# Three hundred trial orders for a two-block kernel, and order edges around the scatters of a sequence

## The chip, the cores and the metric

The kernel runs on one core of a Trainium2 chip. The metric is the device time of one execution in microseconds (us), and the time that counts is the median of several executions. One execution was also taken with the hardware profiler. A core has five engines that work through instruction lists of their own: TensorE (PE) for matmuls, VectorE (DVE), ScalarE (ACT), GpSimd (POOL), and SyncE (SP), which here only issues transfers. Engines wait for one another on semaphores, and each executes its list in order.

## The reference

Sixteen sequences of 512 tokens of width 128 pass through two blocks. Each block is an attention and a mixture of eight experts, with a layer norm after each of the four steps:

```python
x = L0_attn_x                                    # 16 x 512 x 128, fp32
x = layernorm(x + L0_attn(x))                    # 16 heads of 64: cumulative sums of gated values
x = layernorm(x + L0_ffn(x))                     # one of 8 experts for each token (argmax), relu
x = layernorm(x + L1_attn(x))                    # 16 heads of 8: softmax with a position bias
x = layernorm(x + L1_ffn(x))                     # shared expert + one of 8 for each token, silu
```

The first attention forms for each head `cumsum(cross * values) * p2e * extra + values * diag` over a matching denominator, and multiplies by an output weight. The second is a softmax over 512 x 512 scores for each of 16 heads. In both mixtures a token goes to the expert with the largest logit, and to it alone.

## The kernel before, in words

**Tiles.** A sequence is held as four tiles of 128 tokens (NT = 4). The first attention works tile by tile (`tile0`): values `pv` (L894), the gated values `ev` (DVE, L907), their cumulative sums `cum` by a triangular matrix (PE, L929), the division `o` in two DVE steps (L941, L945), a transpose `po` (L952), its copy `ot` on ACT (L955) and the output product `y` (L960). From one tile to the next, the last row of `cum` is copied out (`carry`, ACT, L936) and added into `ev` by a transfer that POOL issues (L920); POOL also computes `self` (L913). The second attention goes round by round over four groups of four heads: bf16 scores `s` (PE, L1127 and L1134) whose row maxima DVE takes (`tops`, L1149), then the scores `st` in fp32 (L1190), bias added on DVE (`p`, L1205), exponential on ACT (L1211), and the product `av` with the values (L1220).

**Mixtures.** Sequences go to the mixtures in chunks of 2, 3, 4, 4, 2 and 1. `route` works out on DVE at which row of a list in DRAM each token stands, sorted by expert. `scatter` then writes the tokens to this list: for each sequence four indirect transfers of 128 rows from POOL (the helper's line is L678). `slots` reads the list back in blocks of 128 rows (`xq`, SP, L756), fetches weights of the block's expert by indirect transfers (`ws`, POOL, L678), runs the expert (up products L1012 or L1385, down products `py` L808) and writes results (L798), and `gather` fetches each token's result (`yg`, POOL).

**What sets the order.** Nothing of this is issued as it is written. Each step is an operation in a plan (`Plan.op`): an engine, a cost and a delay given by hand, the buffers it reads and writes, and a due time. `Plan.order` runs a list scheduler over the operations once: whenever an engine is free in its own clock, it takes the operation with the smallest due time that is ready and has buffers. The kinds of buffers are counted there; the PSUM tiles of two banks, of kind "pair", are three. The instructions are emitted in the order of the plan's starts, and `block_kernel` then ties each emitted instruction to the one before it with an edge of order that asks for no semaphore.

**Around the scatters.** In `scatter`, each of the four transfers waits for the list to be zeroed and for the readers of its former content. For all but the first, the program also states that there is no dependency on any scatter sent so far to this list:

```python
                if t:
                    for other in sent:
                        tc.declare_no_dep(inst, other, reason="rows of their own")
```

These are the same instructions that the edges of order tie one to the next.

Of the kernel before, what the change touches and what calls it, by code (L numbers as in the profile page):

```python
# [2 lines left out]

# [1 line left out]

# [15 lines left out]
NT = N // P  # L21
# [14 lines left out]
VW = 9  # L36
EPS = 1e-5
ROUNDS = NG * NT
EARLY = 1.5

INV2PI = 0.15915494309189535
# [27 lines left out]
class Plan:  # L69
# [33 lines left out]
                buf.left += 1  # L103
        return o

    def order(self):
        free, engines = dict(self.room), range(5)
        leaving = {k: 0 for k in free}
        idle = [0.0] * 5
        able = [[] for _ in engines]  # L110
        unstarted = {}
        for o in self.ops:
            for buf in o.bufs:
                unstarted[buf] = unstarted.get(buf, 0) + 1
            if not o.waits:
                able[o.engine].append(o)
        events, now, out = [], 0.0, []
        self.out, self.freekinds = out, free
        while len(out) < len(self.ops):
            for e in engines:  # L120
                if idle[e] > now:
                    continue
                held = {}
                for o in sorted(able[e], key=lambda o: o.key):
                    if o.ready > now + 1e-9:
                        continue
                    need = {}
                    for buf in o.bufs:
                        if not buf.made:
                            need[buf.kind] = need.get(buf.kind, 0) + 1  # L130
                    if all(
                        free[k] >= n and free[k] + leaving[k] - held.get(k, 0) >= n
                        for k, n in need.items()
                    ):
                        break
                    for k, n in need.items():
                        held[k] = held.get(k, 0) + n
                else:
                    continue
                able[e].remove(o)  # L140
                for k, n in need.items():
                    free[k] -= n
                for buf in o.bufs:
                    if not buf.made:
                        buf.made = True
                        o.makes.append(buf)
                    unstarted[buf] -= 1
                    if not unstarted[buf]:
                        leaving[buf.kind] += 1
                out.append(o)  # L150
                o.start = now
                idle[e] = now + o.cost
                heappush(events, (idle[e], len(out), None))
                heappush(events, (idle[e] + o.delay, len(out), o))
                for then in o.then:

                    pass
            if len(out) == len(self.ops):
                break
            assert events, "no operation can start"  # L160
            now = events[0][0]
            while events and events[0][0] <= now + 1e-9:
                _, _, o = heappop(events)
                if o is None:
                    continue
                for then in o.then:
                    then.waits -= 1
                    then.ready = max(then.ready, now)
                    if not then.waits:
                        able[then.engine].append(then)  # L170
                for buf in o.bufs:
                    buf.left -= 1
                    if not buf.left:
                        free[buf.kind] += 1
                        leaving[buf.kind] -= 1
        self.span = now
        return out


# [1 line left out]
def block_kernel(ctx: ExitStack, tc: tile.TileContext, d, out: bass.AP):  # L181
    nc = tc.nc
# [43 lines left out]
    op = plan.op  # L226
    names, listed = {}, {}
    placed, fetched, zeroed, gathered = {}, {}, {}, {}

    def buf(kind, name):  # L230
        pool, shape, dtype, bufs = kinds[kind]
        return Buf(
            kind, lambda: pool.tile(shape, dtype, tag=kind, name=name, bufs=bufs)
        )

    def load(name, shape, src=None, delay=3.4, gate=()):
# [15 lines left out]
        out=tri, in_=ones, compare_op=ALU.is_ge, fill=0.0, base=0,  # L252
# [5 lines left out]
        out=stri, in_=ones, compare_op=ALU.is_ge, fill=0.0, base=-1,  # L258
# [4 lines left out]
        out=flip, in_=ones, compare_op=ALU.is_equal, fill=0.0, base=1 - P,  # L263
# [31 lines left out]
    for i in range(2):  # L295
# [8 lines left out]
        for pads, k, dtype in ((qk_pad, "qk", F32), (qk16_pad, "qk16", BF16)):  # L304
            m = cp.tile([P, 2, N], dtype, tag=f"{k}_pad{i}", name=f"{k}_pad{i}")
# [13 lines left out]
    def tok(ap):  # L319
        return ap.rearrange("p (t w) -> p t w", w=W)  # L320
# [356 lines left out]
    def indirect(out=None, to=None, in_=None, of=None):  # L677
        nc.gpsimd.indirect_dma_start(  # L678
            out, bass.IndirectOffsetOnAxis(to, 0) if to is not None else None,
            in_, bass.IndirectOffsetOnAxis(of, 0) if of is not None else None,  # L680
        )

    def last():
        return list(nc.cur_bb.bb.instructions)[-1]

    def awaits(inst, others):
        for other in others:
            tc.add_manual_dep(
                inst, other.name,
                mybir.DependencyInfo(mybir.DependencyClass.Sync, mybir.DependencyReason.DATA),  # L690
                reason="list of tokens",
            )

    def scatter(which, c, i, src, place, store):

        n = f"{which}_{c}"
        sent, taken = placed.setdefault(n, []), fetched.get(f"{which}_{c - 2}", [])
        before = [f"zeros{which}_{c % 2}"]  # L700
        before += [f"fetched{which}_{c - 2}_{s}" for s in range(0, SLOTS, 4)]

        def send():
            for t in range(NT):
                indirect(
                    out=store[0], to=place()[:, NT * i + t : NT * i + t + 1],
                    in_=tok(src())[:, t, :],
                )
                inst = last()
                if t:  # L710
                    for other in sent:
                        tc.declare_no_dep(inst, other, reason="rows of their own")
                awaits(inst, [zeroed[f"{which}_{c % 2}"], *taken])
                sent.append(inst)

        op(
            POOL, 5.1, send, reads=[src, place, *before, f"token{n}_{i - 1}"],
            writes=[f"token{n}_{i}"], delay=2.5,
        )
# [336 lines left out]
    def attention1(b, x, at):  # L1056
# [99 lines left out]
        def shifted(g):  # L1156

            pm, mx = buf("one", f"pm_{b}_{g}"), buf("mx", f"mx_{b}_{g}")

            def turn():  # L1160
                for it in range(NT):
                    nc.tensor.transpose(pm()[:NG, col(it)], tops[g % 2][:, it, :], ident)

            op(
                PE, 0.5, turn,
                reads=[("tops", g % 2, it, jp) for it in range(NT) for jp in range(2)],
                writes=[pm],
            )
            op(
                ACT, 0.5, lambda: nc.scalar.copy(mx()[:NG], pm()[:NG]), reads=[pm],  # L1170
                writes=[mx],
            )
            op(
                SP, 0.42,
                lambda: nc.sync.dma_start(qk_pad[g % 2][D1 :: 32, 0, :], mx()[:NG]),
                reads=[mx, *[("qk", g % 2, j) for j in range(4)]],
                writes=[("shift", g % 2)], delay=2.4,
            )
# [77 lines left out]
        for it in range(NT):  # L1256
            plan.due = at - NT - EARLY + it
            maxima(0, it)
        plan.due = at - EARLY
        shifted(0)  # L1260
        for g in range(NG):
            more = g + 1 < NG
            acc = buf("one", f"av_{b}_{g}")
            if more:
                plan.due = at + NT * g - EARLY
                spread(g + 1, qk, qk16)
            for t in range(NT):
                plan.due = at + NT * g + t
                weighted(g, t, acc)
                if more:  # L1270
                    plan.due -= EARLY
                    maxima(g + 1, t)
# [210 lines left out]
    def second(c, b0, xs, lg):  # L1483
        for i, x in enumerate(xs):
            at = float(ROUNDS * (b0 + i))
            attention1(b0 + i, x, at)
# [4 lines left out]
    held = [[] for _ in CHUNKS]  # L1491
# [73 lines left out]
    for c, b0 in enumerate(starts):  # L1565
        begin, length = float(ROUNDS * b0), float(ROUNDS * CHUNKS[c])
        lg = buf("lg", f"lg1_{c}")
# [3 lines left out]
        if c + 1 < len(CHUNKS):  # L1571
# [5 lines left out]
            c, b0, held[c], lg, store,  # L1577
            lambda u: begin + length + (ROUNDS * CHUNKS[c + 1] if c + 1 < len(CHUNKS) else 1) * 0.9 * u,
        )


    order = plan.order()
    block = nc.cur_bb.bb.instructions
    mark = len(block)
    for o in order:
        for made in o.makes:
            made.tile = made.make()
        o.emit()
    chain = [i for i in list(nc.cur_bb.bb.instructions)[mark:]]
    for before, then in zip(chain, chain[1:]):  # L1590
        tc.add_manual_dep(
            then, before.name,
            mybir.DependencyInfo(mybir.DependencyClass.NoSync, mybir.DependencyReason.DATA),
            reason="order",
        )


# [84 lines left out]
```

## Time and profile before

| | |
|---|---|
| median of 3 executions | 2499.63 us (2495.47 to 2499.99) |
| the profiled execution's own time | 2567.31 us |
| its span, first to last instruction | 2564.4 us |
| granted PE clock in it, mean | 0.938 |
| PE busy | 2258.0 us (88%) |
| DVE busy | 1934.8 us (75%) |
| ACT busy | 1000.6 us (39%) |
| POOL busy | 731.2 us (29%) |

The profiler's execution is longer than the timed ones by 2.7%. In the rows of the profile, `out<-in` gives the program's names of what an instruction writes and reads, and L and a number its line. A slice row divides the span in 40 equal parts and gives the busy share of each in tenths. A row of waits says who waited for whom, in us, how many times, and the longest. PE and PEld are the matmuls and the loads of their weights, which overlap.[...]

### The profile page before, as it was taken

Reading aid. Unit: us, or ns where it says so; the run is one execution under the profiler, and the core shown is the slowest. Engines: PE = TensorE matmul, PEld = TensorE weight load, DVE = VectorE, ACT = ScalarE, POOL = GpSimd, SP = SyncE. Lnnn points to the kernel's source line nnn. Section 1 sums busy time; section 2 is a strip of 40 time slices with the busy share of each in tenths; the row PEclk is TensorE's granted clock in tenths of the full one; section 3 lists DMA queues with packets and bytes.
Section 4 is the critical chain, followed back from the end, with each engine's and each line's share of the span. In section 5 each row is a group of like instructions: output and inputs, shape, how many; then the busy total and the mean of one; then the engine's idle time right before and its main releaser. Section 6 shows DMA issues by size and latency. Waiting matters only on the chain.

```text
span 2564.4 us, 33958 instructions
## 1 busy us (share of the span) xinstructions
PE 2258.0 (88%) x12820; PEld 1125.6 (44%) x12820; DVE 1934.8 (75%) x3030; ACT 1000.6 (39%) x1336; POOL 731.2 (29%) x763
## 2 busy tenths in 40 slices
PE   5978889899997997899889988899999889998974
PEld 4556424344553443355434423454344235443443
DVE  5455787897786789777778798778887886789761
ACT  6323144533433543333335443334454333444330
POOL 1244322323223244312132343212213323223232
PEclk9999889999998998898989998999999899998886
DMA  7613113112011331211023411122223112332332
GB/s 179 196 37 101 29 51 90 42 32 75 16 44 52 99 99 30 62 54 41 10 55 102 113 39 46 40 68 70 54 63 90 52 41 74 113 104 62 90 102 88
DMA packets 152438, 179.96 MB, mean 70 GB/s; under 512 B 19332, under 2 KB 125444, under 8 KB 152276
## 3 DMA queue, kind: packets, MB, share of 16 engines
q1 hardware_dynamic: 125588, 84.27, 12.5%
q0 software_dynamic: 26688, 93.53, 12.2%
q8 instruction: 101, 1.65, 0.3%
q14 instruction: 61, 0.50, 0.1%
HBM read 127.67 MB, written 42.93 MB: 67 GB/s over the span
## 4 chain that ended last, share of the span: by engine, by line
PE 58%; DVE 26%; ACT 5%; issue 5%; DMA 2%; another core or an unknown queue 2%; POOL 1%; SPq 0%; DVEq 0%; POOLq 0%; ACTq 0%
PE st L1190 9%; DVE p L1205 9%; PE av L1220 7%; PE s L1127 5%; DVE tops L1149 5%; PE y L960 4%; PE cum L929 4%; PE pv L894 4%; PE s L1134 3%; PE py L808 3%; ACT p L1211 2%; PE po L952 2%; PE pg L1385 2%; DVE o L941 2%
## 5 line engine op out<-in xcount | busy, mean ns | idle before, releaser
L1211 ACT ACTIVATE p<-p 128x1024 f32<-128x1024 f32 x512 | 539.4, 1058 | 539.0 <-DVE p L1205 480.8
L1205 DVE TENSOR_TENSOR p<-st,bias 128x1024 f32<-128x1024 f32 x512 | 606.0, 1216 | 126.1 <-PE st L1190 95.7
L1149 DVE TENSOR_REDUCE tops<-s 128x2 f32<-128x1024 f32 x512 | 604.7, 1215 | 72.5 <-PE s L1134 48.2
L1190 PE MATMUL st<-qk_pad 32*128 32x512 f32 x2048 | 385.2, 663 | 35.6 <-DVE p L1205 20.6
L678 POOL DMA_INDIRECT ws<-tab,rows x212 | 207.6, 979 | 678.9 <-PE py L808 317.8
L1127 PE MATMUL s<-bias,ident 128*128 128x512 bf16 x1024 | 329.4, 403 | 64.0 <-DVE p L1205 37.1
L1220 PE MATMUL av<-p,vaug 128*32 128x512 f32 x2048 | 291.6, 641 | 21.2 <-ACT p L1211 18.2
L913 POOL TENSOR_TENSOR self<-ev,own 128x1024 f32<-128x1024 f32 x64 | 122.6, 1917 | 514.5 <-DVE ev L907 283.7
L1134 PE MATMUL s<-qk_pad 32*128 32x512 bf16 x1024 | 207.0, 397 | 4.1 <-DMA qk_pad<-qk 4.0
L1190 PEld LDWEIGHTS st<-qk_pad 32*128 32x128 f32 x2048 | 113.5, 189 | 190.2 <-issue 70.5
L1127 PEld LDWEIGHTS <-ident 128*128 128x128 bf16 x1024 | 82.3, 99 | 234.6 <-issue 226.4
L678 POOL DMA_INDIRECT yg<-results,place x128 | 126.4, 988 | 141.2 <-issue 46.0
L1134 PEld LDWEIGHTS <-qk_pad 32*128 32x128 bf16 x1024 | 48.8, 91 | 244.2 <-issue 232.9
L929 PE MATMUL cum<-ev,tri 128*128 128x512 f32 x256 | 133.1, 647 | 10.2 <-DVE p L1205 5.1
L960 PEld LDWEIGHTS y<-ow,ot 128*128 128x128 f32 x1024 | 125.6, 197 | 32.8 <-issue 15.2
L960 PE MATMUL y<-ow,ot 128*128 128x128 f32 x1024 | 131.3, 283 | 3.2 <-ACT ot L955 2.6
L894 PE MATMUL pv<-vw,xt 128*128 128x512 f32 x256 | 130.1, 634 | 3.7 <-DVE p L1205 1.9
L941 DVE TENSOR_TENSOR o<-cum,gg 128x1024 f32<-128x1024 f32 x64 | 78.2, 1222 | 68.0 <-PE cum L929 53.2
L808 PEld LDWEIGHTS py<-ws,h 128*128 128x128 f32 x848 | 101.8, 195 | 36.2 <-DVE h L1309 14.4
L907 DVE TENSOR_TENSOR ev<-pv,ex 128x1024 f32<-128x1024 f32 x64 | 78.0, 1220 | 51.6 <-PE pv L894 45.3
L808 PE MATMUL py<-ws,h 128*128 128x128 f32 x848 | 111.2, 285 | 6.3 <-DVE h L1309 5.3
L952 PE MATMUL po<-ident,o 128*128 128x128 f32 x512 | 72.0, 286 | 36.7 <-DVE o L945 30.8
(189 smaller groups left out, 2757.0 us busy)
## 6 DMA issues: line engine op xcount, KB each, us to landing
xq<-tokens SPq DMA_DIRECT2D x44, 256.0 KB
results<-yq SPq DMA_DIRECT2D x44, 256.0 KB
qk_pad<-qk SPq DMA_DIRECT2D x256, 32.0 KB
slid<-line SPq DMA_DIRECT2D x16, 448.0 KB
tokens<-zero SPq DMA_DIRECT2D x4, 1472.0 KB
xt<-in_xt SPq DMA_DIRECT2D x16, 256.0 KB
x<-in_x SPq DMA_DIRECT2D x16, 256.0 KB
qk_pad<-qk SPq DMA_DIRECT2D x256, 16.0 KB
```

The costliest lines, as they stand in the source:

```text
L678: nc.gpsimd.indirect_dma_start(out, bass.IndirectOffsetOnAxis(to, 0) if to is not None else None, in_, bass.IndirectOffsetOnAxis(of, 0) if ...
L808: nc.tensor.matmul(py()[:, col(s)], h()[:, c, col(s)], ws[s]()[:, off + c * W : off + (c + 1) * W], start=(c == 0), stop=(c == 1),)
L894: nc.tensor.matmul(pv()[:, hf, :], xt()[:, col(t)], vw[:, hf * N : (hf + 1) * N], start=True, stop=True,)
L929: nc.tensor.matmul(cum()[:, hf, :], tri, ev()[:, hf, :], start=True, stop=True)
L960: nc.tensor.matmul(y()[:, :P], ot()[:, hf, col(c)], ow[:, 4 * hf + c, :], start=(hf == 0 and c == 0), stop=(hf == 1 and c == 3),)
L1127: nc.tensor.matmul(s()[:, i, :], ident16, bias16[:, 4 * g + 2 * jp + i, 2 * u + 1 : 2 * (u + N) : 2], start=True, stop=False,)
L1134: nc.tensor.matmul(s()[:, i, :], pad[r, 0, col(it)], pad[r, 1, :], start=False, stop=True,)
L1149: lambda s=s, jp=jp: nc.vector.tensor_reduce(tops[g % 2][:, it, 2 * jp : 2 * jp + 2], s(), AX.X, ALU.max, negate=True,),
L1190: nc.tensor.matmul(s[jp]()[:, i, :], pad[r, 1, col(jt)], pad[r, 0, :], start=True, stop=True,)
L1205: lambda jp=jp, h=h, pj=pj: nc.vector.tensor_tensor(pj(), s[jp](), bias[:, h : h + 2, u : u + N], ALU.add),
L1211: ACT, 1.0, lambda pj=pj: nc.scalar.activation(pj(), pj(), AF.Exp),
L1220: nc.tensor.matmul(acc()[32 * j : 32 * j + 32, :], va[:, jt, h * VW : h * VW + 32], p[j // 2]()[:, j % 2, :], start=(jt == 0), stop=(jt == ...
```

## The change

First, the scheduler is split. `listed(keys)` is the list scheduler as before, taking one key for each operation; it works on indices for speed, and returns the starts, or None if nothing can start. `order` calls it with the due times, and then 300 times (TURNS) with keys made from the starts of the list kept so far. In turn 0 they are those starts themselves. In every other turn a stretch of the plan's clock of 30, 100 or 300 is drawn, and in it either single operations (2, 10 or 30% of them), each by an amount of its own, or all operations of one kind by one amount are moved, by up to 2.4, 8 or 24. The new list is kept if the plan's span is not longer. No operation, cost, delay, buffer or due time is changed, and the draw has a fixed seed. Operations that start at the same time are now emitted by engine.

Second, in `scatter` the statement that there is no dependency is kept among the four transfers of a sequence only, and each of the four waits for the four of the sequence before (`sent[-NT:]`). When the edges of order are made, the four count as one member of the chain: each of them is tied to all of the member before and the member after, and they are not tied to one another.

```diff
+TURNS, SHIFT = 300, 8.0
...
+        start = self.listed([o.key[0] for o in ops])
+        best, draw = span(start), Random(0)
+        kinds_of = [o.emit.__code__ for o in ops]
+        for turn in range(TURNS):
+            width, by = draw.choice((30.0, 100.0, 300.0)), SHIFT * draw.choice((0.3, 1.0, 3.0))
+            low = draw.uniform(-width / 2, best)
+            one, share = kinds_of[draw.randrange(len(ops))], draw.choice((0.02, 0.1, 0.3))
+            same, single = draw.uniform(-by, by), draw.random() < 0.5
+            keys = list(start)
+            for i, t in enumerate(start) if turn else ():
+                if low < t < low + width:
+                    if single:
+                        if draw.random() < share:
+                            keys[i] += draw.uniform(-by, by)
+                    elif kinds_of[i] is one:
+                        keys[i] += same
+            other = self.listed(keys)
+            if span(other) <= best:
+                start, best = other, span(other)
+        self.span = best
+        out = sorted(ops, key=lambda o: (start[place[o]], o.engine))
...
         def send():
+            before, row = sent[-NT:], []
             for t in range(NT):
...
-                if t:
-                    for other in sent:
-                        tc.declare_no_dep(inst, other, reason="rows of their own")
-                awaits(inst, [zeroed[f"{which}_{c % 2}"], *taken])
-                sent.append(inst)
+                for other in row:
+                    tc.declare_no_dep(inst, other, reason="rows of their own")
+                awaits(inst, [zeroed[f"{which}_{c % 2}"], *taken, *before])
+                row.append(inst)
+            sent.extend(row)
+            for inst in row:
+                together[inst.name] = row
...
-    chain = [i for i in list(nc.cur_bb.bb.instructions)[mark:]]
+    chain = []
+    for i in list(nc.cur_bb.bb.instructions)[mark:]:
+        row = together.get(i.name, [i])
+        if i is row[0] or i.name == row[0].name:
+            chain.append(row)
     for before, then in zip(chain, chain[1:]):
-        tc.add_manual_dep(
-            then, before.name,
+        for a in before:
+            for b in then:
+                tc.add_manual_dep(
+                    b, a.name,
```

More of the change, by code (lines that the diff above doesn't have):

```diff
@@ L1 @@
+from bisect import insort
 from contextlib import ExitStack
 from heapq import heappop, heappush
+from random import Random
 import numpy as np
@@ L104, in op, with listed @@
         return o
[L106 to L121, printed above, removed]
+    def listed(self, keys):
+        free = [self.room[k] for k in self.kinds]
+        soon = list(free)
+        ops, n = self.ops, len(self.ops)
+        cost, delay, engine, bufs = self.costs, self.delays, self.engines, self.uses
+        kind, then = self.kind, self.thens
+        waits, left, begin = list(self.waiting), list(self.users), list(self.users)
+        made = [False] * len(kind)
+        able = [[] for _ in range(5)]
+        for i in range(n):
+            if not waits[i]:
+                able[engine[i]].append((keys[i], i))
+        for a in able:
+            a.sort()
+        idle, events, now, start, done = [0.0] * 5, [], 0.0, [0.0] * n, 0
+        look = [True] * 5
+        while True:
+            for e in range(5):
+                if idle[e] > now or not look[e]:
@@ L122, in order @@
                     continue
[L123 to L126, printed above, removed]
+                held, pick, line = {}, -1, able[e]
+                for q, (_, i) in enumerate(line):
                     need = {}
-                    for buf in o.bufs:
-                        if not buf.made:
-                            need[buf.kind] = need.get(buf.kind, 0) + 1
+                    for b in bufs[i]:
+                        if not made[b]:
+                            need[kind[b]] = need.get(kind[b], 0) + 1
@@ L131, in order @@
                     if all(
-                        free[k] >= n and free[k] + leaving[k] - held.get(k, 0) >= n
-                        for k, n in need.items()
+                        free[k] >= m and soon[k] - held.get(k, 0) >= m
+                        for k, m in need.items()
                     ):
+                        pick = q
                         break
-                    for k, n in need.items():
-                        held[k] = held.get(k, 0) + n
-                else:
+                    for k, m in need.items():
+                        held[k] = held.get(k, 0) + m
@@ L139, in order @@
+                if pick < 0:
+                    look[e] = False
                     continue
[L140 to L158, printed above, removed]
+                i = line.pop(pick)[1]
+                for b in bufs[i]:
+                    k = kind[b]
+                    if not made[b]:
+                        made[b] = True
+                        free[k] -= 1
+                        soon[k] -= 1
+                    begin[b] -= 1
+                    if not begin[b]:
+                        soon[k] += 1
+                        look = [True] * 5
@@ L159, in order @@
+                start[i] = now
+                done += 1
+                idle[e] = now + cost[i]
+                heappush(events, (idle[e], done, -1 - e))
+                heappush(events, (idle[e] + delay[i], done, i))
+            if done == n:
                 break
-            assert events, "no operation can start"
+            if not events:
+                return None
             now = events[0][0]
             while events and events[0][0] <= now + 1e-9:
-                _, _, o = heappop(events)
-                if o is None:
+                i = heappop(events)[2]
+                if i < 0:
+                    look[-1 - i] = True
@@ L165, in order @@
                     continue
[L166 to L176, printed above, removed]
+                for t in then[i]:
+                    waits[t] -= 1
+                    if not waits[t]:
+                        insort(able[engine[t]], (keys[t], t))
+                        look[engine[t]] = True
@@ new lines, in listed, with order, span @@
+                for b in bufs[i]:
+                    left[b] -= 1
+                    if not left[b]:
+                        free[kind[b]] += 1
+                        look = [True] * 5
+        return start
+    def order(self):
+        ops, place, bufs = self.ops, {}, []
+        for i, o in enumerate(ops):
+            place[o] = i
+        number = {}
+        for o in ops:
+            for b in o.bufs:
+                if b not in number:
+                    number[b] = len(bufs)
+                    bufs.append(b)
+        self.kinds = sorted(self.room)
+        self.kind = [self.kinds.index(b.kind) for b in bufs]
+        self.users = [b.left for b in bufs]
+        self.uses = [[number[b] for b in o.bufs] for o in ops]
+        self.thens = [[place[t] for t in o.then] for o in ops]
+        self.waiting = [o.waits for o in ops]
+        self.costs, self.delays = [o.cost for o in ops], [o.delay for o in ops]
+        self.engines = [o.engine for o in ops]
+        def span(start):
+            return max(t + o.cost for t, o in zip(start, ops)) if start else float("inf")
+        start = self.listed([o.key[0] for o in ops])
+        assert start is not None, "no operation can start"
+        best, draw = span(start), Random(0)
[18 more added lines that the diff above has]
+        out = sorted(ops, key=lambda o: (start[place[o]], o.engine))
+        for o in out:
+            o.start = start[place[o]]
+            for b in o.bufs:
+                if not b.made:
+                    b.made = True
+                    o.makes.append(b)
@@ L228, in block_kernel @@
     placed, fetched, zeroed, gathered = {}, {}, {}, {}
+    together = {}
     def buf(kind, name):
@@ L1588, in block_kernel @@
         o.emit()
-    chain = [i for i in list(nc.cur_bb.bb.instructions)[mark:]]
-    for before, then in zip(chain, chain[1:]):
-        tc.add_manual_dep(
-            then, before.name,
-            mybir.DependencyInfo(mybir.DependencyClass.NoSync, mybir.DependencyReason.DATA),
-            reason="order",
-        )
+    chain = []
[3 more added lines that the diff above has]
+            chain.append(row)
+    for before, then in zip(chain, chain[1:]):
+        for a in before:
+            for b in then:
+                tc.add_manual_dep(
+                    b, a.name,
+                    mybir.DependencyInfo(
+                        mybir.DependencyClass.NoSync, mybir.DependencyReason.DATA
+                    ),
+                    reason="order",
+                )
 def _pad_heads(w):
```

## The prediction

> **What bounds the kernel now.** I read first the busy shares by slice, then a table of three stretches cut where the trace shows the first and last matmul of the second attention (L1220, "av"), then the waits of TensorE (PE) in those stretches. The slices:
>
> ```profile
> PE   5978889899997997899889988899999889998974
> DVE  5455787897786789777778798778887886789761
> POOL 1244322323223244312132343212213323223232
> PEclk9999889999998998898989998999999899998886
> ```
>
> PE stands at 8 or 9 tenths in most slices and VectorE (DVE) at 7 or 8; GpSimd (POOL) is two thirds idle. The stretches; the first two figures are the stretch and its length, then busy us of PE, PE weight load, DVE, ScalarE (ACT) and POOL, then the granted clock:
>
> ```profile
> 0.00:326.20 326.20, 260.87 (x1243) 175.27 (x1243) 187.71 (x350) 111.74 (x147) 102.79 (x120) 0.92 0.38 107
> 326.20:2472.00 2145.80, 1954.80 (x11376) 916.30 (x11374) 1720.56 (x2593) 879.34 (x1174) 595.58 (x607) 0.95 0.23 64
> 2472.00:2564.40 92.40, 42.37 (x203) 34.01 (x203) 26.51 (x88) 9.54 (x15) 32.87 (x36) 0.71 0.31 94
> ```
>
> PE's idle time is 65.3 us at the start, 191.0 in the long middle and 50.0 in the tail, 306.4 in all. The work is the same after the change, so an order can only win from these. In the tail one sequence runs alone through its experts, a chain without other work to put beside it; an order can do little there. The longest waits of PE in the middle, with total, times and longest:
>
> ```profile
> PE s L1127 <- DVE p L1205: 37.1, 48, 3.4
> PE st L1190 <- DVE p L1205: 20.6, 22, 5.6
> PE av L1220 <- ACT p L1211: 18.2, 30, 1.4
> PE s L1127 <- DVE tops L1149: 13.9, 22, 2.3
> ```
>
> The first, second and fourth are one kind. The matmul that fills a score tile waits until DVE has read an older one: PSUM holds three tiles of kind "pair", shared by both attentions and both experts. They are many and short (0.8 us on average): not one late transfer, but PE work and DVE work arriving in lumps. With six smaller rows of that kind (cum and pv and po and ph on p, po on tops, pu_m on tops: 5.1, 1.9, 1.6, 1.4, 2.1, 2.9) it is 86.6 us. The third kind is latency: the product of the weights asks for an exponential that has just begun. At the start the largest is
>
> ```profile
> PE po L952 <- DVE o L945: 25.4, 11, 5.0
> ```
>
> the transposes of the first attention, issued too close behind the cumulative sums.
>
> **What the Trainium skill says.** "Perfetto Trace Analysis", Identifying the Most-Contended Engine, warns that busy matmul time is a poor measure of headroom, and Optimization Strategy says to look for what ends the gaps of the engine that binds, and that a gap repeated over a stretch can mean too few SBUF or PSUM buffers. The trace agrees: PE is 91% busy in the middle, with weight loads at 43%, and its gaps end with the release of "pair" tiles. The change adds no buffer; it can only space their use. "DMA: Bandwidth & Descriptors", Two DMAs through the same engine are not ordered, says that the issuing engine has to wait for the first transfer's semaphore before a dependent one; the added edges make POOL do that. Its section on the anatomy of a DMA from GpSimd gives a fixed 2.0 us, mostly the write's receipt, as the price of such a wait. The trace has no row for it, but the next lines bound it.
>
> **The change, part by part.** Part one, the scatters. Of a sequence's four scatters to the token list, three are bound by no order edge in the built program and run ahead; the fourth stays in its planned place. For a chunk of four sequences POOL shows (start, duration, idle before):
>
> ```profile
> 801.29 0.96 POOL L678 DMA_INDIRECT tokens<-x,place  x1 [0.30 <-issue]
> 802.56 0.95 POOL L678 DMA_INDIRECT tokens<-x,place  x1 [0.30 <-issue]
> 809.02 0.99 POOL L678 DMA_INDIRECT ws<-tab,rows  x1 [5.50 <-PE py L808]
> ...
> 814.07 1.00 POOL L678 DMA_INDIRECT tokens<-x,place  x1 [0.30 <-issue]
> ```
>
> and SyncE's queue then
>
> ```profile
> 818.03 0.93 SPq L756 DMA_DIRECT2D xq<-tokens  x2
> ```
>
> So the last scatter stood 10.2 us behind its place (814.07 less 802.56 and one step of 1.27), behind four weight fetches, and the fetch of the lists went out 2.96 us after it ended. In the chunk of one sequence it is 1.3 us (2501.3 to 2502.57). After the change four scatters stand together, and the first of each next sequence waits until the four before have landed: chunks of 2, 3, 4, 4, 2 and 1 sequences, in two layers, make 20 such places. In the new order 14 of them have nothing between, so POOL stands still for 1.3 to 3.0 us: 18 to 42 us for the 14, and 26 to 60 if all 20 stand. Behind them on POOL are the products "self" (L913), the carry transfers (L920) for which PE's cumulative sums wait, the rsqrt of the layer norms and the weight fetches. I cost both sides at nothing: for the gain, PE waits for a list transfer only 7.9 us in all, 6.9 of it in the tail where a single sequence has no second row; for the loss, POOL is busy 595.58 of 2145.80 us in the middle (28%). If that cover is missing, up to 60 us.
>
> Part two, the search. It keeps each operation, cost and buffer, and moves places: of 1876 neighbouring pairs on PE only 664 stay neighbours, with a mean shift of 4 places, 171 at most. DVE, ACT, POOL and SyncE are moved with it, as are their transfers. I take no time from the plan's own clock. What I can count is how much PE work the two orders put between a producer and its consumer, at the trace's durations (cum 2.08 us, pv 2.03, po 1.12, y 2.05, s 1.05, st 1.50, av 1.14), against what the round trip needs where the trace shows it shortest:
> - cum to po over two DVE operations (1.22 and 1.29) needs 2.75 us. The old order is short in 10 of 64 places, by 18.3 us in sum, the new one in 6, by 7.0: 11.3 won.
> - po to y over ACT needs 1.16: 2.4 to 0, 2.4 won. pv to cum needs 2.45: 1.8 to 0.4, 1.4 won.
> - st to av over DVE and ACT needs 3.6: 10.2 to 15.9, 5.7 lost.
> - "pair" tiles: three fills hand DVE or ACT three readings of 1.2 us, so three fills within less than 3.6 us of PE work must stall. The old order has 227 of these among 1361, short by 152.6 us, the new one 201, by 130.8: 14% less. At least 14% of the traced 86.6 us is won, 12.4; one for one it is 21.8, as more stalls than those named are of this kind. I take 17, between the two.
>
> The sum is 11.3 + 2.4 + 1.4 - 5.7 + 17 = 26.4 us. The profiled execution took 2567.3 us (span 2564.4), so 2541 for such a one; the timed median of 2499.63 is 0.974 of it, which makes 25.7 and 2474. Where PE stalls less, DVE is next: it is busy 80% of the middle.
>
> **Rivals.**
> A, the forecast: 2474, with its own range of 2458 to 2494.
> B, larger: the count sees loops that begin and end on PE, and not lumps on DVE or ACT alone, nor the 20.9 us of middle waits that no release explains. If twice the amount comes, about 50 us, it is 2448. For it: ACT p waits 480.8 us on DVE p, so work does come in lumps. Against: the tail's 50 us and nearly all the start's first 65 don't move.
> C, no change: gaps move instead of closing, since the search fits places to fixed durations, while in the trace PE's clock alone varies between 0.88 and 1.00 from one 100 us to the next. One hundredth of clock on 2258 us of PE is 23 us, all of the gain. Against: 0.95 is the mean of the middle with its gaps, and nothing says that fewer gaps lower it. The time: 2500.
> D, slower, by the waits at the scatters. At 3.0 us a place the gain of 26.4 is used up when 9 of the 20 hold back a carry or a list on PE's path. With the 14 that have nothing between: 42 - 26.4 = 15.6 lost, or 2515. For it: POOL executes in order, and carry is a link of PE's chain. Against: "cum <- DMA ev<-carry" is 2.4 us in the whole trace.
> That the change does nothing is excluded by the orders.
>
> **How the numbers follow.** A has 0.58, B 0.18, C 0.07, D 0.17. A measurement of this kernel tells about 0.2% (5 us) from no change, so faster is A and B, 0.76, same C, 0.07, slower D, 0.17. The range runs from 2440, B with a little more than its doubling, to 2510, 12 places of the 20 at 3.0 us less the gain; beyond it stay about 0.06 below and 0.11 above.
>
> **What would show it.** The table of stretches: the middle's PE idle falls from 191 to about 170 and PE busy stays within 20 us; start and tail keep theirs within 10. "po <- DVE o" falls by about half, the rows of "pair" by a seventh or more. POOL gets rows of scatters in fours with a gap of 1.3 to 3.0 us before the next four; "cum <- carry" stays below 6 us. It is wrong if PE's busy time rises with a lower clock (C), if carry or list waits on PE pass 25 us (D), or if the middle shrinks by over 40 us (B).

## The result, and the profile after

The kernel after takes 2470.71 us (median of 4 executions, 2468.43 to 2474.68). The kernel before took 2499.36 us in the same comparison (4 executions, 2495.47 to 2499.99). The ratio is 0.9871, with a 95% interval of 0.9848 to 0.9894: faster by 28.7 us, or 1.3%. The profiled execution of after took 2471.01 us, with a span of 2469.3.

The busy shares by slice, of after:

```profile
PE   6978899999998998899989998999999989897974
DVE  6465698898788787878787899888978987688761
POOL 1234521224123252321123341321203333224331
PEclk9999989999999997999999989999999899998986
```

PE has more nines and DVE more eights than before, and the clock row has fewer eights. The table of stretches, cut again at the first and last "av" matmul:

```profile
0.00:342.24 342.24, 282.87 (x1312) 184.31 (x1312) 211.42 (x382) 114.59 (x151) 125.99 (x140) 0.90 0.38 109
342.24:2377.03 2034.79, 1904.27 (x11308) 901.56 (x11306) 1700.31 (x2561) 876.00 (x1170) 576.47 (x587) 0.96 0.23 66
2377.03:2469.30 92.27, 41.59 (x203) 33.51 (x203) 26.31 (x88) 9.55 (x15) 32.87 (x36) 0.71 0.32 94
```

PE's idle time is now 59.4, 130.5 and 50.7 us, against 65.3, 191.0 and 50.0: nearly all of the fall is in the middle. The start is longer by 16 us because the search put 69 more matmuls before the first "av" (1312 against 1243), so busy time has to be compared in sum: 2228.7 us against 2258.0, for the same 12820 matmuls. The matmuls themselves took 29.3 us less, for which the forecast has no term. The largest waits of PE in the middle:

```profile
PE av L1284 <- ACT p L1275: 21.8, 27, 6.0
PE s L1191 <- DVE p L1269: 17.7, 33, 1.3
PE st L1254 <- DVE p L1269: 12.7, 17, 2.8
PE s L1191 <- DVE tops L1213: 11.7, 29, 2.3
PE st L1254 <- DVE tops L1213: 10.9, 7, 5.7
```

The wait for a "pair" tile that DVE still reads fell from 37.1 to 17.7 us, and the wait for the exponential is now the longest. The last row was 1.0 us before. At the start:

```profile
PE po L1016 <- DVE o L1009: 10.2, 8, 2.8
```

It was 25.4 us. These rows look like the forecast. But one thing in the profile of before doesn't fit its own times: that execution took 2567.31 us where the timed ones took 2495 to 2500. It is not one of the timed ones, as the profiled execution is for every other kernel here, and the record does not say on which chip it ran. It holds a kind of row that the prediction did not read, waits whose releaser is called "remote": the awaited signal came at a time when the trace shows nothing ending that would send it. Three such rows of before, over its whole span:

```profile
ACT us L1231 <- remote: 17.6, 2, 12.3
DVE tops L1149 <- remote: 12.2, 4, 5.0
DVE p L1205 <- remote: 12.1, 5, 4.6
```

One by one, waits of DVE and ACT on "remote" come to 67.3 us in before, in 16 places; the profile of after has none. The experiments had to say what these are, and which half of the change removes them.

In three later comparisons, each on a chip of its own, before took 2568 to 2586 us and after 2502 to 2515. The record does not name the chip of the first comparison, so whether the chip makes this difference is not shown; each number below is read against the before of its own comparison.

### The profile page after: what moved, and what is told of

Its sections match the earlier page's. It is cut to its first block, busy times and chain, and to the rows that moved or that the text cites. A ratio compares the mean times of both kernels' runs of the same rounds, so it can differ in the third digit from the quotient of the medians.

```text
span 2469.3 us, 33955 instructions
## 1 busy us (share of the span) xinstructions
PE 2228.7 (90%) x12820; PEld 1119.4 (45%) x12820; DVE 1938.0 (78%) x3030; ACT 1000.1 (41%) x1336; POOL 735.3 (30%) x763
## 3 DMA queue, kind: packets, MB, share of 16 engines
q8 instruction: 101, 1.65, 0.3%
## 4 chain that ended last, share of the span: by engine, by line
PE 60%; DVE 26%; issue 5%; ACT 4%; POOL 2%; DMA 2%; SPq 1%; DVEq 0%; POOLq 0%; ACTq 0%
PE st L1254 9%; DVE p L1269 8%; PE av L1284 7%; DVE tops L1213 6%; PE s L1191 6%; PE cum L993 4%; PE s L1198 4%; PE py L872 3%; PE pv L958 3%; PE y L1024 3%; PE po L1016 2%; PE ph L1076 2%; PE pg L1449 2%; PE pu L1449 2%; DVE o L1005 1%
## 5 line engine op out<-in xcount | busy, mean ns | idle before, releaser
L1254 PE MATMUL st<-qk_pad 32*128 32x512 f32 x2048 | 369.2, 665 | 24.9 <-DVE p L1269 12.7
L1284 PE MATMUL av<-p,vaug 128*32 128x512 f32 x2048 | 285.8, 628 | 22.1 <-ACT p L1275 21.8
L1234 ACT COPY mx<-pm 4x512 f32<-4x512 f32 x64 | 36.6, 572 | 178.1 <-PE pm L1226 177.9
```

The lines of the kernel that those rows point to most:

```text
L1254: nc.tensor.matmul(s[jp]()[:, i, :], pad[r, 1, col(jt)], pad[r, 0, :], start=True, stop=True,)
L1284: nc.tensor.matmul(acc()[32 * j : 32 * j + 32, :], va[:, jt, h * VW : h * VW + 32], p[j // 2]()[:, j % 2, :], start=(jt == 0), stop=(jt == ...
```

## The experiments

My theory was that the search wins all of it and that the edges at the scatters cost nothing on either side. The first rival was the opposite split; then, once the first runs were in, the question was how the scatters can matter at all.

**First comparison: one part alone.** Before stood at 2583.22 us (2566.98 to 2598.52) here. Before once more, unchanged:

> The kernel before, unchanged, for a second profile. The first profiled execution took 2567 us against timed ones of 2495 to 2500, and the one of the kernel after 2471 against 2468 to 2475. If the first profile was only a slow draw, this one has a span near 2497 us, and the middle (first to last product of the second attention) keeps its number of waits but loses some 60 us of PE's busy and idle time together. If being profiled makes this order slower, it is near 2564 again.

It took 2582.89 us, ratio 0.9988 (0.9969 to 1.0007): two equal programs differ by 0.1%.

The new scatters alone, with the search turned off:

```diff
-TURNS, SHIFT = 300, 8.0
+TURNS, SHIFT = 0, 8.0
```

> The order of before (no turn of the search), with the scatters of a sequence together and the landing wait between sequences. Theory (the search alone makes the gain; the scatters are hidden): 2499 us, within 5. Rival 1 (the gain comes from scatters that are no longer late): 2471 to 2480. Rival 2 (landing waits cost, and the search pays for them): 2505 to 2520.

It took 2520.7 us, ratio 0.9761 (0.9731 to 0.979). That is 62.5 us faster from the part that I had costed at nothing. Apart from the scatters the engines' lists are nearly those of before: by the names in the traces, 49 of PE's 12820 places hold another matmul, and two places each of DVE and ACT another instruction.

The search alone, with the scatters of before:

```diff
-            before, row = sent[-NT:], []
...
-                for other in row:
-                    tc.declare_no_dep(inst, other, reason="rows of their own")
-                awaits(inst, [zeroed[f"{which}_{c % 2}"], *taken, *before])
-                row.append(inst)
-            sent.extend(row)
-            for inst in row:
-                together[inst.name] = row
+                if t:
+                    for other in sent:
+                        tc.declare_no_dep(inst, other, reason="rows of their own")
+                awaits(inst, [zeroed[f"{which}_{c % 2}"], *taken])
+                sent.append(inst)
```

> The new order of issue with the scatters as before: three of four bound by no order edge, no landing wait between sequences. Theory: 2471 us, within 5. Rival 1 (scatters make the gain): about 2495. Rival 2 (landing waits cost): 2455 to 2465.

It took 2564.98 us, ratio 0.9925 (0.9896 to 0.9954): 18.2 us, and by the interval 12 to 27, which holds the 25.7 that I had for it.

Both parts, but of the 300 turns only turn 0, in which the scheduler is given its own starts as keys:

```diff
-TURNS, SHIFT = 300, 8.0
+TURNS, SHIFT = 1, 8.0
```

> One turn instead of 300: the list is made once more with the starts of the first list as its keys, and nothing is moved. Scatters as after. In the plan's own units, which are no time of the chip, this alone makes 17 of the 50 that the whole search makes. If the chip follows the plan in proportion, 17/50 of 28.7 us: 2489. If only the random moves count: 2499. If the replay is what matters and the moves fit only the plan's fixed durations: 2471.

It took 2516.72 us, ratio 0.9752 (0.9721 to 0.9783), within 4 us of the scatters alone. Here the theory fell: the scatters make the larger part, and the two parts (62.5 and 18.2 us) don't add up to what after gains in any comparison (28.7, 70.2 and 65.6 us).

**What the scatters do.** The trace of before's repeat shows one place. First what DVE, ACT, POOL and PE did there, by start time, with duration and the idle time ahead of it in brackets:

```profile
347.38 1.15 PE L1190 MATMUL st<-qk_pad 32*128 32x512 f32 x8
348.39 0.25 DVE L988 TENSOR_TENSOR l_m<-lg,m 128x96 f32<-128x96 f32 x1
350.56 0.59 ACT L1231 COPY us<-av 128x512 f32<-128x512 f32 x1 [5.40 <-remote]
...
355.07 0.97 POOL L678 DMA_INDIRECT tokens<-x,place  x1 [0.30 <-issue]
356.31 1.23 DVE L1205 TENSOR_TENSOR p<-st,bias 128x1024 f32<-128x1024 f32 x1 [7.67 <-remote]
357.57 1.06 ACT L1211 ACTIVATE p<-p 128x1024 f32<-128x1024 f32 x1 [6.24 <-issue]
```

POOL sends twelve scatters in a row here, one every 1.27 us. PE's "st" matmuls ended at 348.53, yet `p`, which reads them, began on DVE only at 356.31, after 7.67 us idle; the trace has PE's update of the semaphore at 356.22. DVE had run an instruction without a wait at 348.39, and PE its next matmuls at 351.20, so between them both engines took up work. By these rows it is PE's signal that came late. The ends of matmuls are modelled in this trace, though, so it cannot tell a late signal from matmuls that ended later than it draws them; "late signals" below stands for either. While all stood, the clock fell too. The same place in windows (length, then busy time of each engine as above, and the clock), in before's repeat and then with the new scatters alone:

```profile
352.00:358.00 6.00, 1.32 (x6) 0.49 (x6) 1.23 (x1) 0.43 (x1) 3.13 (x4) 0.64 0.15 46
358.00:364.00 6.00, 5.11 (x16) 0.83 (x18) 5.17 (x7) 3.80 (x4) 0.00 (x0) 0.50 0.00 1
```

```profile
352.00:358.00 6.00, 6.00 (x39) 1.72 (x38) 5.77 (x7) 2.48 (x3) 3.57 (x4) 1.00 0.14 45
```

PE works 1.32 of 6 us where it otherwise works all 6 (about one per cent of PE's records is missing in both traces, but DVE and ACT stand as well), and then goes on at half clock. The Trainium skill, "TensorE: Matmul & The Clock Gate", What's actually happening, says that an idle window of about 3.4 us puts the clock at half; the trace agrees (0.50 after the pause), so this pause costs twice.

That this is where the time goes can be summed. The 512 `p` instructions of DVE stand in the same order in before and in the kernel with the scatters alone, so the difference of their start times is a running lag. Between the profile of before (span 2564.4) and that of the scatters alone in the third comparison (2519.5) it grows by 49.6 us; 48.5 us of it arise between 4 us before and 10 us after a run of scatters, stretches that make about a seventh of the span, and 1.1 us elsewhere. Of the 16 places in before's trace where DVE or ACT ends a wait on "remote", 14 have seven or more scatters started in the 12 us before, which is so for 4% of the span. This shows where the time goes, and not yet by what.

The Trainium skill, "Runtime: NRT & Kernel Launch", Instruction fetch mechanics, offers another cause: instructions come in blocks of 256, and a block could be late behind the scatters' traffic. The profile of before speaks against it: of its eleven waits on "remote" that are over 2 us, six have no packet of the instruction queues that starts in them or in the 4 us ahead, and none in that trace took more than 1.52 us. Why PE's signals are late stays open.

**Second comparison: how many may be in flight.** Before stood at 2585.53 us (2567.46 to 2604.74). After unchanged:

> The kernel after, unchanged, beside the next three. In the last comparison the old order with the scatters held back took 2520.7 us where the kernel before took 2583; the new order should take some 25 to 45 us less than the held-back old one, so 2475 to 2495 where before is 2583 (or 2471 where before is 2499). No pause of DVE or ACT that no release explains is longer than 7 us.

It took 2515.35 us, ratio 0.9744 (0.9697 to 0.9792).

After without the waits for landing; a sequence's four still count as one member of the chain:

```diff
-            before, row = sent[-NT:], []
+            row = []
...
-                for other in row:
+                for other in [*sent, *row]:
...
-                awaits(inst, [zeroed[f"{which}_{c % 2}"], *taken, *before])
+                awaits(inst, [zeroed[f"{which}_{c % 2}"], *taken])
```

> The kernel after with the scatters still together and in their planned places, but without the landing wait between sequences: up to 16 scatters follow one another. Theory (many scatters in flight hold up TensorE's signals, and with them all engines): 40 to 75 us slower than after, about as slow as the new order with the old scatters, and the pauses of DVE, ACT and PE without a release come back within the rows of scatters. Rival (what cost time was the fourth scatter out of its place, and the missing edges of order): as fast as after, within 5 us. Rival (the landing wait is only a cost on POOL): 0 to 10 us faster than after.

It took 2556.82 us, ratio 0.9881 (0.9828 to 0.9934); without its longest execution, of 2584.52 us, the median is 2553.48. Some 38 us of the gain are gone, and the rows are back:

```profile
DVE p L1269 <- remote: 18.6, 6, 6.1
DVE tops L1213 <- remote: 18.4, 4, 7.3
```

So it is mostly the wait that wins, not the new place in the chain. Waiting for the sequence before the last, so that up to eight are in flight:

```diff
-            before, row = sent[-NT:], []
+            before, row = sent[-2 * NT : -NT], []
...
-                for other in row:
+                for other in [*sent[-NT:], *row]:
```

> The kernel after where the four scatters of a sequence wait for those of the sequence before the last: at most eight in flight. If the pauses grow with the number in flight, between after and the kernel without landing waits: 10 to 40 us slower than after. If they set in only above eight, as after.

It took 2554.24 us, ratio 0.9899 (0.9853 to 0.9945), no better than no wait. Waiting for every single scatter:

```diff
-                for other in row:
-                    tc.declare_no_dep(inst, other, reason="rows of their own")
-                awaits(inst, [zeroed[f"{which}_{c % 2}"], *taken, *before])
+                awaits(inst, [zeroed[f"{which}_{c % 2}"], *taken, *before, *row])
```

> The kernel after where each scatter waits for the landing of the one before, also inside a sequence: one in flight, 116 places with a wait instead of 20. At 1.3 to 3.0 us each this adds 96 waits, 125 to 290 us of POOL. If POOL's idle time hides waits as I assumed, within 10 us of after, or faster by some us, as four in flight may still hold up a signal. If landing waits reach PE's path, 30 us slower or more.

It took 2603.4 us, ratio 1.0077 (1.0051 to 1.0103). Its waits:

```profile
POOL tokens L739 <- DMA tokens<-xs_m,place: 101.2, 53, 4.5
POOL tokens L739 <- DMA tokens<-x,place: 99.9, 54, 4.1
PE pts L845 <- DMA xq<-tokens: 67.4, 8, 14.1
```

POOL stands 201.1 us in 107 waits, 1.88 us each, and now PE waits 67.4 us for lists that come late. So with no limit, eight, four and one in flight the times are 2553, 2554, 2515 and 2603 us, and the waits of DVE and ACT on "remote" come to 93.9, 87.5, 18.4 and 2.5 us. Of the values tried four is the fastest: most of the late signals are gone, and the landing waits do not yet reach PE as rival D has it.

**Third comparison: the search on top of the scatters.** Before stood at 2568.11 us (2553.21 to 2573.86). The scatters alone (no turns) and after, both again:

> The old order with the scatters held back, now beside the new order in one comparison. If before is near 2584: 2518 to 2523 as last time. If before is near 2499, as where the kernel after took 2471: about 2471 if the scatters make the gain there too, about 2499 if the search makes it.

> The kernel after beside the one with the scatters alone. If the search is worth what the two comparisons so far say, 3 to 8 us faster than the scatters alone; my count in the prediction says 26.

They took 2517.0 us, ratio 0.981 (0.9774 to 0.9847), and 2502.47 us, ratio 0.9755 (0.9722 to 0.9788). The search is worth 14.5 us here, though the two intervals just overlap. Then another draw of the search, and more turns:

```diff
-        best, draw = span(start), Random(0)
+        best, draw = span(start), Random(1)
```

> The search with another seed of the draw: another order, with a plan's span of 2400.9 of its own units against 2400.0. If the span in these units tells the time, within 3 us of after. If the order matters in ways that the plan does not hold, 5 to 20 us away from it, either way.

```diff
-TURNS, SHIFT = 300, 8.0
+TURNS, SHIFT = 2000, 8.0
```

> 2000 turns instead of 300: the plan's span falls from 2400 to 2382 of its own units. If the chip follows in the proportion of the search so far (about 5 us for 50 units on these chips): 2 us less than after. If it follows one for one: 18 us less. If the search only fits the plan's fixed durations: no different or slower.

They took 2494.11 us, ratio 0.9721 (0.9689 to 0.9752), and 2491.79 us, ratio 0.9716 (0.9683 to 0.9749): 23 and 25 us better than the scatters alone, and ahead of after in the same comparison, though the intervals of the ratios overlap. The plan's own span does not foretell this: 2450.5 for the scatters alone, 2433.3 with one turn, 2400.0 for after, 2400.9 for the other draw, 2382.0 for 2000 turns. The other draw has after's span and is 8 us faster; 2000 turns shorten the plan by 18 units more and the kernel by 2 us.

PE's waits with the scatters alone, in the middle and (last row) at the start:

```profile
PE s L1191 <- DVE p L1269: 31.6, 44, 3.3
...
PE av L1284 <- ACT p L1275: 16.8, 30, 1.4
...
PE st L1254 <- DVE tops L1213: 1.0, 3, 0.6
...
PE po L1016 <- DVE o L1009: 25.2, 11, 5.0
```

and the same of after on the same chip:

```profile
PE s L1191 <- DVE p L1269: 25.4, 34, 4.8
PE av L1284 <- ACT p L1275: 22.5, 25, 5.9
...
PE st L1254 <- DVE tops L1213: 10.2, 7, 5.6
...
PE po L1016 <- DVE o L1009: 10.2, 8, 2.8
```

These two kernels differ by the search alone, so the forecast's terms can be held against them one by one. "po" gives 15.0 us. The nine rows of "pair" tiles that the forecast summed fall from 77.4 to 63.1 us. But "st" on "tops" is of the same kind: a score tile waits until DVE has read an older one. The forecast left it out at 1.0 us, and it rises to 10.2, so the kind as a whole gives about 5 us. Two waits make most of the new row, 3.0 us near 769 and 5.6 us near 1289; the first trace of after has the same two (3.0 and 5.7 us), so they belong to the order. "av" loses 5.7 us, and the two small terms, "y" on "ot" and "cum" on "ev", give 1.8 and 0.7. That is about 17 us in sum, where the time fell by 14.5. The nearness is partly luck: PE's idle time as a whole falls by 7.7 us only (271.1 to 263.4), so other waits took back the rest, and its busy time falls by 5.8 us.

With the other draw PE is idle for 243.4 us, with 2000 turns for 239.5: 27.7 and 31.6 us less than with the scatters alone, about the size that the forecast named. One candidate for the 8 to 11 us between them and after is the late signals: waits on "remote" ahead of DVE and ACT come to 27.8 us in this trace of after, to 8.6 and 8.0 in theirs. In after some stand behind four to seven scatters, three with none near, and two of the places (about 1320 and 2158 us) recur in the trace of after from the second comparison; what else delays a signal there was not tried. But the sum of these waits does not foretell the time by itself: with the scatters alone it is 25.1 us in the first comparison and 5.6 in the third, at the same span of 2519.5 us. So this cause is not shown.

## Why the prediction was right or wrong

The time came out 3 us under the forecast, but in the three later comparisons most of the gain is where the forecast had put nothing.

**The scatters: "I cost both sides at nothing" failed.** It asked what may wait for a scatter: the list, the carry, POOL's own queue. On those it was close. The 17 landing waits in after,

```profile
POOL tokens L739 <- DMA tokens<-x,place: 15.0, 9, 3.9
POOL tokens L739 <- DMA tokens<-xs_m,place: 13.1, 8, 2.7
```

are 1.65 us each in the mean. Five of them are 0.30 us, the gap between any two scatters, and so no wait; the other twelve are 1.0 to 3.9 us, 2.2 in the mean, ten of them inside the 1.3 to 3.0 of the forecast. The Trainium skill, "DMA: Bandwidth & Descriptors", anatomy of one DMA, gives a fixed 2.0 us, and the traces are near it (2.2 here, 1.88 with one in flight). PE's wait for lists went from 7.9 to 12.5 us, "cum" on "carry" from 2.4 to 0.6. What the forecast did not ask is what a long run of scatters does to work that has no part in it. The rows of waits on "remote" were there. The forecast passed over them, and called the 2.7% between the profiled and the timed executions of before a scale. With the scatters alone the gain is 62.5 and 51.1 us in two comparisons.

**The search: 26.4 us was too much for this order, and the "pair" term is the one that was mis-sized.** Term by term (foretold, then measured with the scatters held): "po" 11.3, 15.0; "pair" 17, about 5; "av" −5.7, −5.7; the two small ones 3.8, 2.5. The rows that the forecast listed fell by 14.3 us, but a row of the same kind that was nearly nothing in before took 9.2 us back. The time moved 14.5, 23 and 25 us for three orders with the scatters held, and 18.2 with the old ones. Between the second comparison's after and the first one's scatters alone it is only about 4 us (0.9744 against 0.9761). The loops that the forecast counted are real, and "po" and "av" show it; how much time closing them wins varies from order to order.

**Why the total still fitted** is not settled. In the forecast's comparison before took 2499 us and not 2568 to 2586, and after gained 28.7 us, close to the count for the search. That fits an account in which the timed executions of before had few late signals there, and only the profiled one, at 2567, had them. The profile of after from that comparison fits it too: it has no wait on "remote", where the two later profiles of the same kernel have 18.4 and 27.8 us. The two parts were not run apart in that comparison, so it stays open, and with it whether 2471 came by the forecast's way or by luck.

**Rivals.** D (slower by landing waits) has a real mechanism: with one scatter in flight the kernel is slower than before. With twelve such waits it isn't reached. B asked for twice the amount and for a middle shorter by over 40 us. That sign of being wrong came: the profiled middle is shorter by 111 us (2145.80 to 2034.79). It does not speak for B's amount, which the time excludes: 16 us of it are work moved to the start, and the rest is set against an execution of before that was itself 68 us above its timed ones. C (gaps move, the clock eats the gain) did not come: the clock of the middle went from 0.95 to 0.96 and busy PE fell.

**The signs.** Middle idle was to fall to about 170; it fell to 130.5, and to 157.7 by the scatters alone and 152.0 by both in the third comparison. PE busy was to stay within 20 us in the middle: it fell by 50.5, of which 22.0 went to the start, where 69 more matmuls stand; in sum it fell by 29.3, so this sign did not hold. With the scatters alone PE is busy for 2248.4 us. The start's and the tail's idle stayed within 10 (59.4, 50.7). "po" fell by more than half and the nine "pair" rows, 86.6 to 55.7 us, by more than a seventh; with "st" on "tops" it is 87.6 to 66.6, still more than a seventh, against that same execution of before. The scatters stand in fours; this is one gap with the scatters alone:

```profile
777.55 0.96 POOL L739 DMA_INDIRECT tokens<-x,place  x1 [0.30 <-issue]
780.65 0.96 POOL L739 DMA_INDIRECT tokens<-x,place  x1 [2.14 <-DMA tokens<-x,place]
```

## What to carry to other kernels

When a profiled execution stands some per cent above the timed ones, ask first whether it is one of them, and look in it for what they may not have, before using it as a scale: here waits whose releaser the trace could not name were the hint. A transfer can cost engines that never wait for it, so price a burst by what the other engines do while it lasts, and try a limit on how many are in flight at more than one value. A count of work between producer and consumer on one engine foretold the direction of each wait that it covered, but a new order also makes waits that the old profile hardly shows: sum a kind of wait over all its rows after the change, and not over those that were large before. What the time then does needs a run, and the planner's own span ranked the orders only roughly.

## What was not expected of the hardware

- With seven to sixteen indirect scatters of 128 rows sent 1.27 us apart, signals of PE reached DVE and ACT late, by 5 to 12 us at single places, with 50 us lost in a kernel of 2564. In the five traces with eight or more in flight the waits on "remote" come to 67.3 to 93.9 us; in the eight with at most four, to 0 to 29.5; with one, to 2.5.
- At the place shown PE went on at half clock (0.50) after such a pause, which adds to its price.
- Between comparisons the same program differed by 3.5% (2499 and 2586 us for before), and by 1.8% (2471 and 2515 us) for after; the three whose chips are on record, for before, by 0.7% (2568 to 2586).
